# Second graph layer: the weights of two source tiles masked in one operation, scores made three steps ahead

## The chip, the core and the metric

The kernel runs on one core of a Trainium2 chip. The metric is the device time of one execution in microseconds (us). The engines are named as in the profile: PE (TensorE, matrix products), PEld (its weight loads), DVE (VectorE), ACT (ScalarE), POOL (GpSimd) and SP (the queue that issues most of the DMAs). Each engine works through its own instructions in order, and waits on semaphores for the others.

## The reference

The input has 3327 nodes with 256 features (padded in the kernel to 26 tiles of 128 rows) and a dense 0/1 adjacency matrix. Two layers follow each other; each is a graph step and a step on the rows alone (a mixture of experts in the first layer, an attention block in the second). The change touches the graph step of the second layer only:

```python
def _L1_gnn_ref(x, adj, W, a):
    Wh = x @ W
    e_src = Wh @ a[:d_out]
    e_dst = Wh @ a[d_out:]
    e = jax.nn.leaky_relu(e_src[:, None] + e_dst[None, :], 0.2)
    mask = (adj > 0) | jnp.eye(N, dtype=bool)
    e = jnp.where(mask, e, NEG_INF)
    alpha = jax.nn.softmax(e, axis=1)
    return alpha @ Wh

x = x + _L1_gnn_ref(_layernorm(x, axis=-1), adj, L1_gnn_W, L1_gnn_a)
```

For every pair of nodes there is a score, a mask from the adjacency matrix, an exponential, and the weighted sum of the rows `Wh`.

## The kernel before

**The stage.** `graph1` first makes `Wh` for all 26 tiles (`wh`, with a column of ones behind, so that the sum of the weights comes out of the same product). Then it walks over the matrix: `steps` lists the pairs (b, j), with b one of seven blocks of up to four target tiles (the last block has two) and j one of the 26 source tiles, j running fastest. That makes 182 steps. All of a step's work is in four small functions, and the loop at lines 747 to 772 calls them with leads of different length.

**A step's four parts.** `weights(k)` (line 681) makes a tile u of 128 x 512 (128 x 256 in the last block): one DVE operation adds the source's term `d8` to the block's first row, and takes the maximum with the block's second row, which is the leaky ReLU; then ACT takes the exponential in place, with `d2` as its bias. The two rows `bcast[b]` are the same on all partitions and are made once for a block. `masked(k)` (line 692) is one DVE operation that compares the adjacency panel with zero and takes the minimum with u: where there is no edge, the weight is 0. Its result is the tile p. `gather(k)` (line 703) is up to four products on PE, p of each target tile against `wh` of the source tile, summed over the 26 steps in PSUM (one accumulator for each target tile). u and p each have four buffers (`ep`, line 617).

**The leads.** Each engine's instructions are issued in the order of the program (`InOrder`). In step k the loop issues `weights(k + 2)`, then `masked(k + 1)`, then `gather(k)`. So on DVE the order is u, p, u, p, and the two scores of the next steps are under way when a step is masked.

**What else shares the engines.** For each tile of the next block `top` (a custom DVE operation over 128 x 1664, twice a tile) finds the largest source term among its neighbours; ACT makes its input with a `Sign` (`sign`, same width). `top` runs in the odd steps 1 to 15 (in block 5 only 1 to 7, as block 6 has two tiles), `sign` two or three steps earlier. `finish` closes a tile of the block before in the steps 1 to 4: a reciprocal and one DVE operation that waits for PE's last product of that tile, then a DMA issued by POOL. `shifts`, at step 16, makes the shift of the next block with small DVE operations, and POOL makes `dg` from it; at step 18 PE multiplies it (`rows`), at step 21 ACT copies it out (`spread_rows`). `panel` loads four source tiles of the adjacency matrix with up to four DMAs on SP, and POOL puts ones on the diagonal where the panel holds one. From block 3 on, POOL also prepares a table (`igw`) for the stage that follows.

## Time and profile before

| what | value |
|---|---|
| median of 6 runs | 2937.1 us (2934.43 to 2941.73) |
| the profiled execution | 2938.11 us, of which the span of the profile is 2936.4 us |
| the stage of the 182 steps | from 622.1 us (first u) to 974.5 us (last product) |
| u on DVE, 128x512 / 128x256 | 156 and 26 operations, 788 and 491 ns each on average |
| exponential of u on ACT, 128x512 / 128x256 | 156 and 26 operations, 718 and 508 ns |
| p on DVE, 128x512 / 128x256 | 156 and 26 operations, 740 and 438 ns |
| `top` on DVE in the stage | 44 operations, 1914 ns |
| `sign` on ACT in the stage | 44 operations, 1574 ns |
| products of `gather` on PE | 1352 passes (676 products of two passes), 310.0 us busy |

Times are of one execution. In the rows of the profile, `out<-in` names the tiles, `xN` counts, and the number in brackets is the idle time of the engine before the row and what ended it. All rows carry line 61, because a helper there issues every instruction; the tile names tell them apart: `u<-bc,d` is the score, `u<-u,d` its exponential, `p<-pan,u` the masking, `sg<-sg,dst` is `top`, `acc<-wh,p` the products. An instruction's duration reaches a little over the start of the next one on the same engine.

### The profile page before, as it was taken

Reading aid. Unit: us, or ns where it says so; the run is one execution under the profiler, and the core shown is the slowest. Engines: PE = TensorE matmul, PEld = TensorE weight load, DVE = VectorE, ACT = ScalarE, POOL = GpSimd, SP = SyncE. Lnnn points to the kernel's source line nnn. Section 1 sums busy time; section 2 is a strip of 40 time slices with the busy share of each in tenths; the row PEclk is TensorE's granted clock in tenths of the full one; section 3 lists DMA queues with packets and bytes.
Section 4 is the critical chain, followed back from the end, with each engine's and each line's share of the span. In section 5 each row is a group of like instructions: output and inputs, shape, how many; then the busy total and the mean of one; then the engine's idle time right before and its main releaser. Section 6 shows DMA issues by size and latency. Waiting matters only on the chain. (4 is left out here: it accounts for less than half of the span.)

```text
span 2936.4 us, 125324 instructions
## 1 busy us (share of the span) xinstructions
PE 2650.9 (90%) x53422; PEld 1961.6 (67%) x53422; DVE 2397.7 (82%) x5619; ACT 1810.7 (62%) x5128; POOL 973.4 (33%) x1448
## 2 busy tenths in 40 slices
PE   7999998879989798999999999999999999999995
PEld 5878887757767666666666666666666666666664
DVE  5102643589999587889989999999999999999997
ACT  6420135555554477777777777777667767676774
POOL 6441634522142146544334323323122222122121
PEclk9999989999999799999999999999999999999998
DMA  9994568647775232333333433333333433433332
GB/s 378 358 328 137 186 206 279 206 177 265 269 243 181 71 91 78 115 99 114 117 100 112 121 110 113 113 115 115 117 112 113 118 111 115 120 113 109 116 110 78
DMA packets 258189, 449.70 MB, mean 153 GB/s; under 512 B 58817, under 2 KB 156609, under 8 KB 257505
## 3 DMA queue, kind: packets, MB, share of 16 engines
q1 hardware_dynamic: 245536, 417.50, 45.3%
q0 software_dynamic: 6576, 18.02, 1.6%
q8 instruction: 421, 6.90, 1.0%
q10 hardware_dynamic: 5520, 6.18, 0.7%
q14 instruction: 136, 1.11, 0.1%
HBM read 393.37 MB, written 25.88 MB: 143 GB/s over the span
## 5 line engine op out<-in xcount | busy, mean ns | idle before, releaser
L61 ACT ACTIVATE sc<-sc,anmax 128x512 f32<-128x512 f32 (+3 forms) x1568 | 1039.8, 668 | 108.6 <-DVE anmax L61 108.5
L61 PEld LDWEIGHTS po<-sc,vr 32*64 32x64 f32 x43728 | 660.1, 130 | 389.2 <-DVE sc L61 233.6
L61 PE MATMUL po<-sc,vr 32*64 32x128 f32 x43728 | 761.8, 275 | 112.7 <-DVE sc L61 75.6
L61 DVE STREAM_TRANSPOSE sc<-sc 128x2048 f32<-128x2048 f32 (+3 forms) x392 | 816.4, 2083 | 27.1 <-ACT sc L61 26.2
L61 PE MATMUL pqk<-kt,qt 64*128 64x512 f32 (+1 forms) x2944 | 737.7, 582 | 21.0 <-ACT qt L61 6.8
L61 DVE TENSOR_SCALAR_CACHE_REDUCE sc<-pqk 128x512 f32<-128x512 f32 (+2 forms) x1152 | 654.9, 622 | 49.1 <-PE pqk L61 47.6
L61 PEld LDWEIGHTS pqk<-kt,qt 64*128 64x128 f32 x2944 | 298.5, 186 | 233.0 <-issue 102.5
L61 PE MATMUL acc<-wh,p 128*128 128x259 f32 x1352 | 310.0, 387 | 34.8 <-DVE p L61 34.7
L61 PEld LDWEIGHTS acc<-wh,p 128*128 128x128 f32 x1352 | 254.2, 190 | 92.9 <-DVE p L61 52.4
L61 PE MATMUL acc<-y,pan 128*128 128x256 f32 x1352 | 302.5, 384 | 11.2 <-DMA pan<-in_adjt_dram 9.4
L61 POOL TENSOR_TENSOR ot<-ot,sxd 128x512 f32<-128x512 f32 x83 | 105.7, 1274 | 584.2 <-ACT ot L61 572.2
L61 ACT ACTIVATION_READ_ACCUMULATOR sc<-sc,anmax 128x1 f32 x1568 | 298.9, 191 | 0.0
L61 PEld LDWEIGHTS acc<-y,pan 128*128 128x128 f32 x1352 | 257.4, 192 | 52.1 <-issue 16.8
L61 DVE CUSTOM_DVE_ANT_0 sc<-pqk,mask 128x512 f32<-128x512 f32 (+3 forms) x416 | 242.2, 636 | 23.5 <-PE pqk L61 23.0
L61 ACT ACTIVATE u<-u,d 128x512 f32<-128x512 f32 (+1 forms) x182 | 125.2, 688 | 159.5 <-DVE u L61 159.4
L61 DVE SCALAR_TENSOR_TENSOR u<-bc,d 128x512 f32<-128x512 f32 (+1 forms) x182 | 135.6, 746 | 0.1
L61 DVE SCALAR_TENSOR_TENSOR p<-pan,u 128x512 f32<-128x512 f32 (+1 forms) x182 | 126.9, 697 | 10.3 <-PE acc L61 6.2
L61 ACT ACTIVATE junk<-ar 128x1664 bf16<-128x1664 f32 x52 | 82.7, 1591 | 64.9 <-DMA ar<-in_adj_dram 63.7
L61 ACT COPY qkv<-ptO 128x256 f32<-128x256 f32 x104 | 38.3, 368 | 133.9 <-PE ptO L61 133.7
L61 PE MATMUL ptO<-igw,ot 128*128 128x68 f32 x832 | 116.6, 283 | 4.1 <-issue 2.4
L61 PEld LDWEIGHTS ptO<-igw,ot 128*128 128x128 f32 x832 | 101.6, 192 | 22.9 <-issue 16.9
L61 DVE CUSTOM_DVE_ANT_0 sg<-sg,dst 128x1664 bf16<-128x1664 bf16 (+2 forms) x56 | 99.7, 1788 | 1.2 <-ACT dst L61 1.0
(340 smaller groups left out, 3027.5 us busy)
## 6 DMA issues: line engine op xcount, KB each, us to landing
vr<-vs SPq DMA_DIRECT2D x976, 128.0 KB
ar<-in_adj_dram SPq DMA_DIRECT2D x104, 832.0 KB
vr<-vs SPq DMA_DIRECT2D x544, 96.0 KB
pan<-in_adjt_dram SPq DMA_DIRECT2D x156, 256.0 KB
pan<-in_adjt_dram SPq DMA_DIRECT2D x26, 1024.0 KB
pan<-in_adjt_dram SPq DMA_DIRECT2D x20, 832.0 KB
w1e<-w SPq DMA_DIRECT2D x59, 256.0 KB
took<-places SPq DMA_DIRECT2D x59, 129.0 KB
```

The costliest lines, as they stand in the source:

```text
L61: made = make(*args, **kw)
```

## The change

Two steps now share one tile of u and one of p, both of shape 128 x 4 x 2 x 128: target tile, which of the two steps, target row. `weights(k)` fills one half of the shared u, in four pieces of 128 elements (two in the last block); it is still one DVE operation and one exponential for each step. `masked` is called in odd steps only, and masks both halves in one operation of 128 x 1024 (128 x 512 in the last block): the panel already holds the two source tiles side by side. The products take their halves of p. The number of elements on every engine stays as it was.

`weights` moves from two to three steps ahead, so that both halves of u exist when they are masked; before the loop, `weights(2)` is added. u and p have three buffers of the double size (24 KB for each partition in all, 16 KB before).

On DVE the order of two steps with a `top` was u(k+1), p(k), u(k+2), p(k+1), `top`, for k odd in the step of the last three. It is now u(k+2), u(k+3), p(k+1 and k+2), `top`, where u(k+2) is issued in the even step k-1 and the rest in the odd step k. What an even step has besides (`finish` in steps 2 and 4, `shifts` in step 16) stands between the two scores.

```diff
             def weights(k):
                 b, j = steps[k]
                 n = len(blocks[b]) * P
-                u = ep.tile([P, BLK], F32, tag="u", name="u")
+                if j % 2 == 0:
+                    es_[k // 2] = ep.tile([P, 4, 2, P], F32, tag="u", name="u", bufs=3)
+                u = es_[k // 2][:, : n // P, j % 2, :]
+                ab = bcast[b].rearrange("p i (t q) -> p i t q", t=4)[:, :, : n // P, :]
                 nc.vector.scalar_tensor_tensor(
-                    u[:, :n], bcast[b][:, 0, :n], d8[:, j : j + 1], bcast[b][:, 1, :n],
-                    ALU.add, ALU.max,
-                )
-                nc.scalar.activation(u[:, :n], u[:, :n], AF.Exp, bias=d2[:, j : j + 1])
-                es_[k] = u
+                    u, ab[:, 0], d8[:, j : j + 1], ab[:, 1], ALU.add, ALU.max
+                )
+                nc.scalar.activation(u, u, AF.Exp, bias=d2[:, j : j + 1])
 
             def masked(k):
+
                 b, j = steps[k]
                 n = len(blocks[b])
-                p = ep.tile([P, 4, P], F32, tag="p", name="p")
+                p = ep.tile([P, 4, 2, P], F32, tag="p", name="p", bufs=3)
 
                 nc.vector.scalar_tensor_tensor(
-                    p[:, :n, :], pans[b, j // 4][:, :n, j % 4, :], 0.0,
-                    es_.pop(k).rearrange("p (t q) -> p t q", t=4)[:, :n, :], ALU.is_gt, ALU.min,
-                )
-                ps_[k] = p
+                    p[:, :n, :, :], pans[b, j // 4][:, :n, ds(j % 4, 2), :], 0.0,
+                    es_.pop(k // 2)[:, :n, :, :], ALU.is_gt, ALU.min,
+                )
+                ps_[k], ps_[k + 1] = p[:, :, 0, :], p[:, :, 1, :]
...
             weights(0)
             weights(1)
+            weights(2)
             masked(0)
...
-                    weights(k + 2)
+                if k + 3 < len(steps):
+                    weights(k + 3)
                 if k + 3 in when:
                     sign(*when[k + 3])
-                if k + 1 < len(steps):
+                if k + 1 < len(steps) and j % 2:
                     masked(k + 1)
                 gather(k)
```

## The prediction

> **What bounds the kernel now.** I read the page's costliest groups first, to find the stage that the change touches, then the busy time of that stage in windows, then VectorE's (DVE's), ScalarE's (ACT's) and TensorE's (PE's) instructions in order of time.

> ```profile
> span 2936.4 us, 125324 instructions
> L61 PE MATMUL acc<-wh,p 128*128 128x259 f32 x1352 | 310.0, 387 | 34.8 <-DVE p L61 34.7
> L61 DVE SCALAR_TENSOR_TENSOR u<-bc,d 128x512 f32<-128x512 f32 (+1 forms) x182 | 135.6, 746 | 0.1
> L61 DVE SCALAR_TENSOR_TENSOR p<-pan,u 128x512 f32<-128x512 f32 (+1 forms) x182 | 126.9, 697 | 10.3 <-PE acc L61 6.2
> ...
> 676.00:730.00 54.00, 48.30 (x208) 38.39 (x208) 52.93 (x84) 30.00 (x35) 11.67 (x14) 1.00 0.73 255
> 920.80:974.50 53.70, 53.63 (x244) 46.06 (x244) 46.51 (x100) 24.76 (x44) 13.06 (x18) 1.00 0.34 104
> ```

> The stage runs from 622 to 975 us: 182 steps, in seven blocks of 26 (the last half as wide). The window lines give PE, weight loads, DVE, ACT, POOL. In a middle block DVE is busy 52.9 of 54.0 us and PE 48.3: DVE sets the pace. From 920.8 us to the end PE is busy 53.6 of 53.7. So what the stage loses or gains is what DVE loses or gains up to 920.8. Inside a block (DVE, ACT, then PE in a neighbouring stretch):

> ```profile
> 692.44 0.75 DVE L61 SCALAR_TENSOR_TENSOR u<-bc,d 128x512 f32<-128x512 f32 x1
> 693.11 0.68 DVE L61 SCALAR_TENSOR_TENSOR p<-pan,u 128x512 f32<-128x512 f32 x1
> 693.71 0.74 DVE L61 SCALAR_TENSOR_TENSOR u<-bc,d 128x512 f32<-128x512 f32 x1
> 694.37 0.68 DVE L61 SCALAR_TENSOR_TENSOR p<-pan,u 128x512 f32<-128x512 f32 x1
> 694.98 1.88 DVE L61 CUSTOM_DVE_ANT_0 sg<-sg,dst 128x1664 bf16<-128x1664 bf16 x1
> ...
> 693.28 0.72 ACT L61 ACTIVATE u<-u,d 128x512 f32<-128x512 f32 x1 [2.12 <-DVE u L61]
> ...
> 706.87 3.77 PE L61 MATMUL acc<-wh,p 128*128 128x259 f32 x16 [0.58 <-DVE p L61]
> 711.21 3.76 PE L61 MATMUL acc<-wh,p 128*128 128x259 f32 x16 [0.57 <-DVE p L61]
> ```

> One instruction of DVE starts before the last has quite ended, so I price by start to start: 0.66 us for a score (u), 0.60 for a masking (p), 1.81 for a `top` (694.98 to 696.79). Two steps with a `top` cost DVE 2×(0.66+0.60)+1.81 = 4.34, and PE, with 3.76 of work, waits 0.58 in each such pair. Without a `top` DVE needs 2.53 for two steps, and runs ahead until the four p buffers are full:

> ```profile
> 729.65 0.69 DVE L61 SCALAR_TENSOR_TENSOR p<-pan,u 128x512 f32<-128x512 f32 x1 [0.38 <-issue]
> 730.26 0.75 DVE L61 SCALAR_TENSOR_TENSOR u<-bc,d 128x512 f32<-128x512 f32 x1
> 731.42 0.69 DVE L61 SCALAR_TENSOR_TENSOR p<-pan,u 128x512 f32<-128x512 f32 x1 [0.41 <-PE acc L61]
> 733.16 0.69 DVE L61 SCALAR_TENSOR_TENSOR p<-pan,u 128x512 f32<-128x512 f32 x1 [0.39 <-PE acc L61]
> ```

> Here p comes every 1.75 us, the rate of PE. These gaps add up to 5.3 us in the first five blocks (14 of them), DVE's only slack.

> **The change, part by part.**

> *One masking for two steps.* 91 masked operations replace 182, with the same elements. The narrow block has the size that gives the fixed part:

> ```profile
> 957.25 0.41 DVE L61 SCALAR_TENSOR_TENSOR p<-pan,u 128x256 f32<-128x256 f32 x1
> 957.58 0.47 DVE L61 SCALAR_TENSOR_TENSOR u<-bc,d 128x256 f32<-128x256 f32 x1
> ```

> 256 elements take 0.335 us start to start, 512 take 0.602: 0.267 per 256, so 1024 should take 1.136, and a pair saves 1.204-1.136 = 0.07. By the durations (0.41, 0.68) it would be 0.14; at the other end nothing, if the wide form ran no better. I take 0.07. Up to 920.8 some 70 pairs count: -4.9 us (0 to -9.8). [...]

> *The new wait.* This is the price that the diff doesn't show. Before, a masking takes the score whose exponential was issued a whole step earlier: p and the next u lie between, 1.26 us. After, the order on DVE in an odd step is u, masking of two, `top`; the masking needs the exponential of the score just one DVE operation earlier. How long that takes is seen at the stage's first step:

> ```profile
> 622.09 1.42 DVE L61 SCALAR_TENSOR_TENSOR u<-bc,d 128x512 f32<-128x512 f32 x2
> 622.88 1.38 ACT L61 ACTIVATE u<-u,d 128x512 f32<-128x512 f32 x2 [1.22 <-DVE u L61]
> 623.69 0.69 DVE L61 SCALAR_TENSOR_TENSOR p<-pan,u 128x512 f32<-128x512 f32 x1 [0.19 <-issue]
> ```

> u ends 0.74 after its start, ACT starts 0.09 later (693.19 to 693.28 above), runs 0.72 and ends at 623.60 here, p starts 0.09 later: 0.74+0.09+0.72+0.09 = 1.64 after u's start. Two scores keep DVE for 2×0.66 = 1.325. So DVE stands 0.315 us in a pair. Bounds: with no hand-off at all 1.46-1.325 = 0.135; with forms in four pieces a little slower, 0.36. I take 0.315, since each of its parts is a row of this trace. Behind the waiting masking stand `top`, the next score and so ACT's next exponential; PE waits for all of them.

> Where it is filled: in blocks 1 to 5 the `finish` of steps 2 and 4 (0.60) comes between the two scores, and at step 16 `shifts` (1.17) does. Of the 70 pairs 55 keep the wait. Where POOL works on `pan`, `dg` or `igw`, DVE's operations are stretched (0.94 for 0.74 at 676 to 684 us), so a score behind covers more: 0.12 of wait is left. POOL is busy with these some 55 of 300 us, so 10 of the 55: 45×0.315+10×0.12 = +15.4 us.

> ACT itself isn't late: in a pair it has two exponentials and a sign, 0.63+1.49+0.63 = 2.75 of 4.6 us. In the form 128x4x128 u and its exponential write pieces of 128; the nearest row, p itself, reads `pan` in such pieces and is no slower than the flat u (0.60, 0.66). I take nothing; the bound is in a rival.

> *Three pairs of buffers.* DVE may be six steps ahead of PE where it was four. That takes the 5.3 us of gaps away if DVE can use it: after step 17 it gains 3.46-(1.325+0.315+1.136) = 0.68 in a pair, 3.4 over five pairs, which never fills three pairs; so no gaps: -5.3. Being further ahead, `finish` at step 1 comes before PE has closed the old block; following PE's steps of 1.73 from step 18 gives 0.3 us in each of four blocks: +1.2 (0 to +4).

> *Coarser hand-over.* PE gets two steps at once. At the last place where it waits (920.8, step 9 of block 5) it used to have one step ready 0.66+0.60 us ahead of the next. Now it gets both 2.53 later and does them back to back, where it would have been 1.73 on: +0.8, once.

> *Start, loads, rest.* The third score ahead puts 0.66 before the first masking, but the work is needed anyway, and DVE reaches its third u at the same time as before: nothing. The panels, rows and copies are issued at the same steps, so SP's and POOL's queues keep their order, and a panel is released a step earlier; its DMA isn't waited for by DVE now (no such releaser among its waits). Were that cover gone, POOL's diagonal fixes, 1.7 us ahead of their reader at 682.8, would be late first. Nothing of the later stage changes: 0.

> **Sum.** +15.4-4.9-5.3+1.2+0.8 = +7.2 us. The profiled execution took 2938.1 (span 2936.4 and 1.7 around it), so 2945.3; it lies 1.0 above the median of six runs, so against that median 2944.3.

> **The rivals.**

> *The wait is covered, and the kernel is faster.* Place: the masking of two behind the second score. Without it remain -4.9-5.3+0.8+1.2 = -8.2: 2928.9. It decides below about 0.15 us in a pair (55×0.15 = 8.2). For it: the bound without hand-offs is 0.135. Against: 0.09 was seen at both hand-overs. Chance 0.11.

> *The deeper buffers pay: no change.* If DVE got one more step ahead at each of five block ends, PE would begin the stretch with `top` 1.73 richer: -8.6. The waits in that stretch alone (30 pairs, some 8.5), its savings (35×0.07 = 2.5) and +0.8 give +6.8; together -1.8, with 1.2 of `finish` -0.6: 2936.5. For it: the gaps show that DVE is stopped by buffers. Against: 3.4 us of gain isn't enough to fill them. Chance 0.22.

> *Slower still.* Pieces of 128 cost: the 256-element operation on y, written in two pieces, takes 0.484 at least, the flat one 0.471; that is 0.026 per 512, 150 scores 3.9 and longer exponentials 1.4: 2949.6. In the last block a pair costs DVE 0.79+0.37+0.60 = 1.76 against PE's 1.73, so that PE, covered now, might wait up to 1.8: 2951.4. The masking that doesn't save at all (the change then not doing what it says) gives 2949.2. Chance 0.17.

> **How the numbers follow.** The forecast has 0.50. A difference of 0.2%, 5.9 us, is about what a measurement of this kernel can tell. Of the forecast 0.39 lies beyond that and 0.11 below; of the second rival 0.17 is within, 0.04 slower and 0.01 faster; the first is faster; the third slower. Slower 0.60, same 0.28, faster 0.12. Range 2935 to 2953: it takes in the second and third rivals and leaves out the first and a little above. The forecast alone has 2941 to 2949.

> **What would show it.** Between two scores in a row and the wide p an idle of about 0.3 us with ACT's u as releaser, in 50 or more pairs, absent where `finish` or `shifts` lies between the scores; p of 1024 elements near 1.2 us; no p waiting for PE in blocks 0 to 4; PE waiting over 0.8 us in each pair with a `top`; the stage ending some 7 us later, and the later stage as long as before. I am wrong if the idle is under 0.15 us, if PE's waits vanish, or if u's or the exponential's duration moves.

## The result, and the profile after

The changed kernel takes 2946.55 us (median of 38 runs, 2934.47 to 2952.95), the kernel before 2940.95 us in the runs beside them (77 runs): a ratio of 1.0017, 95% interval 1.0011 to 1.0023. That is 5 us slower (3.2 to 6.8). The profiled execution took 2949.97 us.

The costliest groups on the page of the changed kernel (busy us, mean ns of one, then idle time before and its releaser):

```profile
span 2948.3 us, 125048 instructions
L61 PE MATMUL acc<-wh,p 128*128 128x259 f32 x1352 | 313.9, 391 | 37.5 <-DVE p L61 37.4
L61 DVE SCALAR_TENSOR_TENSOR u<-bc,d 128x512 f32<-128x512 f32 (+1 forms) x182 | 131.2, 753 | 0.1
L61 DVE SCALAR_TENSOR_TENSOR p<-pan,u 128x1024 f32<-128x1024 f32 (+1 forms) x91 | 111.8, 1228 | 15.8 <-PE acc L61 4.9
```

91 maskings take 111.8 us where 182 took 126.9, but DVE now stands 15.8 us before them (10.3 before). How much the stage loses, and on which engine, a window shows from the first score to the last place where PE waits for weights (stretch, then busy time of PE, weight loads, DVE, ACT, POOL, then PE's granted clock). The kernel before:

```profile
622.00:920.80 298.80, 264.80 (x1132) 212.62 (x1132) 291.35 (x455) 164.99 (x194) 65.40 (x72) 0.99 0.73 252
```

and the changed kernel:

```profile
623.50:931.50 308.00, 271.36 (x1140) 219.39 (x1140) 291.37 (x388) 166.49 (x196) 71.63 (x72) 0.97 0.71 244
```

The two stretches end 1.73 us apart in PE's work (the changed kernel hands over two steps there, the kernel before one). DVE is busy for the same 291 us, and idle for 16.6 us in place of 7.4. By this count all that was lost is DVE standing still. From the first u to the last reciprocal the stage takes 360.1 us, against 352.6 before: 7.5 more.

Where DVE stands: two steps with a `top`, on DVE of the changed kernel (start, duration):

```profile
696.35 1.41 DVE L61 SCALAR_TENSOR_TENSOR u<-bc,d 128x512 f32<-128x512 f32 x2
697.88 1.22 DVE L61 SCALAR_TENSOR_TENSOR p<-pan,u 128x1024 f32<-128x1024 f32 x1
699.02 1.88 DVE L61 CUSTOM_DVE_ANT_0 sg<-sg,dst 128x1664 bf16<-128x1664 bf16 x1
...
700.83 1.41 DVE L61 SCALAR_TENSOR_TENSOR u<-bc,d 128x512 f32<-128x512 f32 x2
```

with ACT between them:

```profile
697.13 0.72 ACT L61 ACTIVATE u<-u,d 128x512 f32<-128x512 f32 x1 [2.05 <-DVE u L61]
```

The exponential starts 0.78 us after its score and ends at 697.85; the wide masking starts at 697.88, 1.53 after that score, where two scores alone would need 1.325. So it waits 0.21 us, and the pair takes 4.48 us (4.34 before). The same kernel's DVE at the end of a block:

```profile
848.16 1.23 DVE L61 SCALAR_TENSOR_TENSOR p<-pan,u 128x1024 f32<-128x1024 f32 x1 [0.52 <-ACT u L61]
...
851.68 1.22 DVE L61 SCALAR_TENSOR_TENSOR p<-pan,u 128x1024 f32<-128x1024 f32 x1 [0.96 <-PE acc L61]
853.79 0.17 DVE L61 RECIPROCAL rd<-acc 128x1 f32<-128x1 f32 x1 [0.89 <-PE acc L61]
```

The gaps for PE, which I had forecast to vanish, are larger than before: over the first five blocks 3.2 us in front of p, 4.1 in front of the reciprocal of `finish`, and 1.8 in rows like the first one beyond their usual 0.13; together 9.1 against 5.3. PE says why. First the kernel before at step 18 of block 1, then the changed kernel at steps 16 to 18 of block 1 and at step 18 of block 3:

```profile
718.83 2.02 PE L61 MATMUL acc<-wh,p 128*128 128x259 f32 x8 [1.26 <-DVE p L61]
...
717.12 3.76 PE L61 MATMUL acc<-wh,p 128*128 128x259 f32 x16 [0.72 <-DVE p L61]
723.41 2.01 PE L61 MATMUL acc<-wh,p 128*128 128x259 f32 x8 [2.53 <-DVE p L61]
...
837.40 3.57 PE L61 MATMUL acc<-wh,p 128*128 128x259 f32 x8 [2.52 <-DVE p L61]
840.77 2.05 PE L61 MATMUL pb<-dg,ones 128*128 128x512 f32 x4
```

Before step 18 PE stands 2.5 us (1.26 before). DVE hands over the steps 16 and 17 together, and until it hands over 18 and 19 it has a `top`, two scores, `shifts` and a wide masking to do: 6.3 us, for which PE has 3.76 of work. The masking itself is slow here, 1.99 us from start to start (721.29 to 723.28) in place of 1.14, while POOL makes `dg`:

```profile
721.29 2.06 DVE L61 SCALAR_TENSOR_TENSOR p<-pan,u 128x1024 f32<-128x1024 f32 x1
...
720.79 3.46 POOL L61 TENSOR_TENSOR dg<-ident,ab 128x512 f32<-128x512 f32 x2 [27.06 <-DVE ab L61]
```

To the usual 0.72 this adds 0.85, and `shifts` adds its 1.17 less the wait of 0.21 that it covers: 2.53 in all. The start of PE's long uninterrupted stretch is late by this. In blocks 0, 2, 3 and 4, not in block 1, PE also runs at half its clock for a while after the stop (3.57 for 2.01 in the row of block 3; the last section has the clock). In exactly these four blocks p later waits for PE (0.30, then 0.96 three times), and the waits for PE at the end of a block are 1.5 to 2.4 us in sum; in block 1 they are 0.59.

### The profile page after: what moved, and what is told of

Read it like the earlier page. It is cut to its first block, busy times and chain, and to the rows that moved or that the text cites. A ratio compares the mean times of both kernels' runs of the same rounds, so it can differ in the third digit from the quotient of the medians.

```text
span 2948.3 us, 125048 instructions
## 1 busy us (share of the span) xinstructions
PE 2655.1 (90%) x53422; PEld 1967.2 (67%) x53422; DVE 2395.0 (81%) x5528; ACT 1810.6 (61%) x5128; POOL 983.0 (33%) x1448
## 5 line engine op out<-in xcount | busy, mean ns | idle before, releaser
L61 ACT ACTIVATE sc<-sc,anmax 128x512 f32<-128x512 f32 (+3 forms) x1568 | 1039.8, 668 | 108.5 <-DVE anmax L61 108.4
L61 PEld LDWEIGHTS po<-sc,vr 32*64 32x64 f32 x43728 | 660.3, 131 | 394.4 <-DVE sc L61 233.6
L61 PE MATMUL po<-sc,vr 32*64 32x128 f32 x43728 | 763.1, 275 | 118.3 <-DVE sc L61 73.9
L61 DVE STREAM_TRANSPOSE sc<-sc 128x2048 f32<-128x2048 f32 (+3 forms) x392 | 816.5, 2083 | 28.2 <-ACT sc L61 27.4
L61 PE MATMUL pqk<-kt,qt 64*128 64x512 f32 (+1 forms) x2944 | 735.6, 581 | 18.2 <-DVE fgs L61 4.6
L61 DVE TENSOR_SCALAR_CACHE_REDUCE sc<-pqk 128x512 f32<-128x512 f32 (+2 forms) x1152 | 654.9, 623 | 48.4 <-PE pqk L61 46.8
L61 PEld LDWEIGHTS pqk<-kt,qt 64*128 64x128 f32 x2944 | 298.7, 185 | 228.4 <-issue 100.9
L61 PE MATMUL acc<-wh,p 128*128 128x259 f32 x1352 | 313.9, 391 | 37.5 <-DVE p L61 37.4
L61 PEld LDWEIGHTS acc<-wh,p 128*128 128x128 f32 x1352 | 258.4, 193 | 94.3 <-DVE p L61 52.1
L61 PE MATMUL acc<-y,pan 128*128 128x256 f32 x1352 | 303.6, 385 | 11.8 <-DMA pan<-in_adjt_dram 10.1
L61 POOL TENSOR_TENSOR ot<-ot,sxd 128x512 f32<-128x512 f32 x83 | 105.9, 1275 | 585.9 <-ACT ot L61 574.2
L61 ACT ACTIVATION_READ_ACCUMULATOR sc<-sc,anmax 128x1 f32 x1568 | 298.7, 190 | 0.0
L61 PEld LDWEIGHTS acc<-y,pan 128*128 128x128 f32 x1352 | 257.9, 192 | 53.3 <-issue 17.8
L61 DVE CUSTOM_DVE_ANT_0 sc<-pqk,mask 128x512 f32<-128x512 f32 (+3 forms) x416 | 242.2, 637 | 24.6 <-PE pqk L61 24.3
L61 ACT ACTIVATE u<-u,d 128x512 f32<-128x512 f32 (+1 forms) x182 | 124.1, 688 | 167.2 <-DVE u L61 166.6
L61 DVE SCALAR_TENSOR_TENSOR u<-bc,d 128x512 f32<-128x512 f32 (+1 forms) x182 | 131.2, 753 | 0.1
L61 DVE SCALAR_TENSOR_TENSOR p<-pan,u 128x1024 f32<-128x1024 f32 (+1 forms) x91 | 111.8, 1228 | 15.8 <-PE acc L61 4.9
L61 ACT ACTIVATE junk<-ar 128x1664 bf16<-128x1664 f32 x52 | 82.7, 1591 | 65.0 <-DMA ar<-in_adj_dram 63.9
L61 PE MATMUL ptO<-igw,ot 128*128 128x68 f32 x832 | 117.4, 284 | 3.2 <-issue 1.5
L61 ACT COPY qkv<-ptO 128x256 f32<-128x256 f32 x104 | 38.3, 369 | 132.9 <-PE ptO L61 132.7
L61 PEld LDWEIGHTS ptO<-igw,ot 128*128 128x128 f32 x832 | 102.4, 193 | 21.9 <-issue 15.0
L61 DVE CUSTOM_DVE_ANT_0 sg<-sg,dst 128x1664 bf16<-128x1664 bf16 (+2 forms) x56 | 99.7, 1789 | 1.2 <-ACT dst L61 1.0
```

The lines of the kernel that those rows point to most:

```text
L61: made = make(*args, **kw)
```

## The experiments

All runs were compared with the kernel before on the same chip. The whole time moves by more than the effect (the median of the kernel before lay between 2940 and 2951 us from one group of runs to the next), so I read the stage too, from the first u to the last reciprocal of each profile, and profiled the kernel before again to see how far that repeats.

| run | stage, us | pair with `top`, us | PE's stop at `shifts`, us | ratio to before, 95% interval |
|---|---|---|---|---|
| before, twice | 352.6, 352.4 | 4.34 | 1.26 | |
| changed | 360.1 | 4.48 | 2.53 | 1.0017 (1.0011 to 1.0023) |
| e1_four_ahead | 351.8 | 4.27 | 2.52 | 1.0000 (0.9988 to 1.0013) |
| e2_two_masks | 355.3 | 4.34 | 2.60 | 1.0002 (0.9989 to 1.0015) |
| e3_mask_before_score | 398.6 | 5.15 | not read | 1.0156 (1.0135 to 1.0176) |
| e4_shifts_later | 353.1 | 4.49 | 0.72 | 0.9993 (0.9981 to 1.0006) |
| e5_top_between | 351.8 | 4.27 | 2.53 | 0.9998 (0.9986 to 1.0009) |
| e6_top_between_shifts_later | 345.2 | 4.27 | 0.51 | 0.9975 (0.9965 to 0.9986) |
| e7_and_finish_later | 345.5 | 4.27 | 0.50 | 0.9982 (0.9967 to 0.9997) |
| e8_before_shifts_later | 350.4 | 4.34 | 0.78 | 0.9985 (0.9975 to 0.9995) |
| e9_best_with_two_masks | 345.9 | 4.34 | 0.57 | 0.9975 (0.9964 to 0.9986) |
| e10_best_with_two_pairs | 352.5 | 4.27 | 0.51 | 0.9992 (0.9982 to 1.0002) |
| e11_before_six_buffers | 351.4 | 4.34 | 1.27 | 0.9994 (0.9984 to 1.0004) |

**The repeat.**

> The kernel before, profiled once more, on the chip of these runs: how far the stage's length repeats. If it lies within 1 us of 352.6, differences of 2 us between single profiles of the stage mean something, though the whole time moves by several us from run to run.

It took 352.4 us. So I read differences of 2 us between stages. That is shown for the kernel before only, whose PE clock is full (1.00) from 630 us to the end of the stage. Where the clock falls in between (in the changed kernel eight products then take 3.25 to 3.57 us in place of 2.01), the number of falls moves the stage too, and those kernels were profiled once.

**Scores four ahead.** One line of the changed kernel, and `weights(3)` before the loop:

```diff
-                if k + 3 < len(steps):
-                    weights(k + 3)
+                if k + 4 < len(steps):
+                    weights(k + 4)
```

> Scores made four steps ahead instead of three, everything else as in the changed kernel: the score whose exponential the wide masking needs is then two scores old. Theory A (the loss is the wait of the masking for the exponential of the score just before it, 0.21 us in a pair by the changed kernel's trace): the idle before the wide masking goes to 0, a pair with a top falls from 4.49 to 4.28 us (4.34 before), and the kernel is 0.2 to 0.4% faster than before, ratio 0.996 to 0.998. Theory B (the loss is the coarse hand-over: PE gets two steps at once and stands longer): nothing of that changes, ratio stays at 1.001 to 1.002.

The wide masking follows its scores without a wait; DVE in this run:

```profile
702.10 1.42 DVE L61 SCALAR_TENSOR_TENSOR u<-bc,d 128x512 f32<-128x512 f32 x2
703.43 1.22 DVE L61 SCALAR_TENSOR_TENSOR p<-pan,u 128x1024 f32<-128x1024 f32 x1
...
730.09 1.42 DVE L61 SCALAR_TENSOR_TENSOR u<-bc,d 128x512 f32<-128x512 f32 x2 [0.62 <-ACT bc L61]
```

The pair takes 4.27 us and the stage is 8.3 us shorter than the changed kernel's, so the wait is real, as theory A says. But the ratio missed its range: PE's stop is still there, and the next block's first score now waits 0.62 us for its rows (last line), in each of five blocks. Nor is all of the 8.3 the wait. In the changed kernel PE releases the first accumulator of a block 16.20 to 16.44 us after the end of the masking behind `shifts` where its clock fell after the stop (blocks 0, 2, 3 and 4), and 14.76 where it didn't (block 1). In this run it is 16.30 in block 0, 16.45 in block 3 and 14.75 or 14.76 in the other three. From that I take it, as an estimate, that the clock fell after two stops in this profile, against four.

**Two maskings.** The same order, each pair masked in two operations:

```diff
-                nc.vector.scalar_tensor_tensor(
-                    p[:, :n, :, :], pans[b, j // 4][:, :n, ds(j % 4, 2), :], 0.0,
-                    es_.pop(k // 2)[:, :n, :, :], ALU.is_gt, ALU.min,
-                )
+                u = es_.pop(k // 2)
+                for i in range(2):
+                    nc.vector.scalar_tensor_tensor(
+                        p[:, :n, i, :], pans[b, j // 4][:, :n, j % 4 + i, :], 0.0,
+                        u[:, :n, i, :], ALU.is_gt, ALU.min,
+                    )
```

> Order and buffers of the changed kernel, but each pair is masked by two operations of 512 elements, one after the other. Theory A: the first needs an exponential that is long done and takes 0.60 us, so the second doesn't wait: the wait (0.21) goes and the saving (0.07) too, a pair with a top takes 4.34 us again; ratio 0.999 to 1.000. Theory B: PE can begin with the first half 0.6 us sooner, so its stops shrink too, but the wait stays where it was; ratio between 1.000 and 1.0015. A third theory, that the pieces of 128 in score and exponential cost: nothing changes, 1.0015.

The pair is back at 4.34 and the stage 4.8 us shorter. The pieces of 128, the third theory, are thereby cleared of all but little; the ratio decides nothing between A and B.

**The wait made larger.** `masked(k + 1)` is issued ahead of `weights(k + 3)`.

> The suspected wait made larger: in the odd step the wide masking is issued before the newer score, so that no score lies behind the one that it waits for. Theory A: 1.53 us from the score's start to the masking's, of which only 0.7 is work: an idle of 0.8 us in place of 0.13 to 0.2, a pair with a top 4.49+0.66 = 5.15 us; 45 to 55 pairs give +25 to +36 us on the changed kernel, ratio 1.010 to 1.014. Theory B: PE's hand-over is even a little earlier, ratio 1.002 or less.

DVE in this run:

```profile
709.48 1.23 DVE L61 SCALAR_TENSOR_TENSOR p<-pan,u 128x1024 f32<-128x1024 f32 x1 [0.79 <-ACT u L61]
...
714.63 1.23 DVE L61 SCALAR_TENSOR_TENSOR p<-pan,u 128x1024 f32<-128x1024 f32 x1 [0.79 <-ACT u L61]
```

Idle 0.79 us and a pair of 5.15, both as forecast by A; the stage grows by 38.5 us, a little above its range. B falls as the only cause.

**Shifts later.** In the changed kernel, `if j == 16` becomes `if j == 17`, so that `shifts` comes behind the wide masking of that step.

> The small operations that make the next block's shifts go from step 16 (between the two scores) to step 17, behind the wide masking. In the changed kernel PE stands 2.5 us at this place in each of five blocks, and its next products then run at half speed for a time in two of them. Theory A: DVE's work is the same and this pair's wait is no longer covered (+0.2 each, 1 us in all), so nothing or slightly slower: ratio 1.001 to 1.003. Theory B: PE's stop falls from 2.5 to about 1.3 us and the slow products go; 5 x 1.2 us gained, ratio 0.999 to 1.000.

Here A falls as the only cause. PE in this run:

```profile
720.75 3.76 PE L61 MATMUL acc<-wh,p 128*128 128x259 f32 x16 [0.72 <-DVE p L61]
725.24 2.01 PE L61 MATMUL acc<-wh,p 128*128 128x259 f32 x8 [0.72 <-DVE p L61]
727.97 1.13 PE L61 MATMUL pb<-dg,ones 128*128 128x512 f32 x2 [0.72 <-POOL dg L61]
729.42 1.12 PE L61 MATMUL pb<-dg,ones 128*128 128x512 f32 x2 [0.32 <-POOL dg L61]
```

The stop falls by 1.8 us in each of five blocks, 8.9 in all. The half clock doesn't occur behind the stop of block 1 (eight products take 2.01 us), and I take it for gone in the others: the mean clock of PE over 279.6 us from the first score is 0.99, against 0.96 in the changed kernel. From the first product of step 18 to that of step 19 PE took 5.0 to 5.3 us in four blocks of the changed kernel and 3.57 in block 1, so 6.5 go (the expectation had seen two of the four). But PE now waits for POOL's `dg`, and the same stretch takes 5.14 in each block, 7.8 back. That gives 7.6, and the stage is 7.0 us shorter, though DVE's pair is as long as before the move. On DVE no p waits for PE any more in the first five blocks, and `finish` waits 1.2 us in place of 4.1.

**Top between the scores, then both, then finish.** The wait is covered by work that is there anyway: `top` goes from the end of the odd step to the next even step.

```diff
+                if k - 1 in when:
+                    top(*when[k - 1], PARTS[1])
...
-                if k in when:
-                    top(*when[k], PARTS[1])
...
-                    if j == 16:
+                    if j == 17:
                         dg = shifts(b + 1)
-                    if j == 18:
+                    if j == 19:
                         pb = rows(b + 1, dg)
```

The first two parts are the first run, all of it the second; the third moves `finish` two steps on as well.

> The changed kernel with each top moved from the end of its odd step to the next even step, where it lies between the two scores and covers the exponential (1.81 us). From the first score to the last reciprocal the stage took 352.6 us before, 360.1 in the changed kernel, 351.9 with scores four ahead, 353.1 with the shifts later. Theory A (the wait behind the second score): no idle before the wide masking in pairs with a top, 4.28 us for such a pair, and the stage is 6 to 9 us shorter than the changed kernel's, 351 to 354 us. Theory B (coarse hand-over at step 17): PE still stands 2.5 us there, and the stage stays near 360. If both cost, as the runs so far suggest, A's number holds and B's 2.5 us remain visible.

> As the run with top between the scores, and the shifts behind the wide masking of step 17, with PE's product for the rows one step later (step 19) so that it doesn't wait for POOL. If the two costs are separate, their gains add up: 360.1-7-7 = 346 us for the stage, ratio 0.997 to 0.998. If both act through one limit (DVE's sum of work, with gaps where PE stops it), the second brings less than 3 us: 349 to 352.

> As the run before it, and finish moved from steps 1 to 4 to steps 3 to 6, since its reciprocal waits 0.3 to 0.9 us for PE's last products in each block when DVE is further ahead. If these waits are slack that DVE has anyway, nothing changes; if they are lost, 5 x 0.5 to 0.9 = 2.5 to 4.5 us are gained: a stage of 342 to 345 us if the run before it takes 346.

The first shortens the stage by 8.3 us and leaves PE's 2.5, as A said; the second takes another 6.6 off. So the two moves add up. The 8.3 again holds more than the wait: the mean clock over 279.6 us from the first score is 0.97 in place of 0.96, and up to step 9 of block 5 DVE waits 4.9 us for PE in place of 7.3. DVE in the second:

```profile
699.20 0.75 DVE L61 SCALAR_TENSOR_TENSOR u<-bc,d 128x512 f32<-128x512 f32 x1
699.87 1.22 DVE L61 SCALAR_TENSOR_TENSOR p<-pan,u 128x1024 f32<-128x1024 f32 x1
701.00 0.75 DVE L61 SCALAR_TENSOR_TENSOR u<-bc,d 128x512 f32<-128x512 f32 x1
701.66 1.89 DVE L61 CUSTOM_DVE_ANT_0 sg<-sg,dst 128x1664 bf16<-128x1664 bf16 x1
```

In a pair with a `top` no idle is left. This version is faster than the kernel before, 2933.5 us against 2940.25, and with that than the changed one. Moving `finish` brought nothing: in the second run its reciprocal doesn't wait in blocks 1 to 5, so there was nothing to gain, and the run doesn't show whether such waits are slack.

**What the gain consists of.** Four controls: the shifts later in the kernel before; the best version with two maskings; the best version with `bufs=2` for p; and the kernel before with `bufs=6` for p.

> A control on the kernel before: single maskings, scores two ahead, but shifts at step 17 behind the masking and the rows' product at step 19, as in the best version so far (stage 345.2 us, against 352.6 and 352.4 in two profiles of the kernel before). If the place of the shifts is a gain of its own, without the merged masking, the stage falls to 348 or less. If it only repairs what the pairs broke, the stage stays at 352 to 354: PE gets one step there as it did, and DVE's work is the same.

> The best version so far (top between the scores, shifts at step 17, three pairs of buffers) with each pair masked by two operations of 512 elements: what the merge alone is worth once neither wait nor hand-over costs. By the rows of 0.60 and 1.14 us, 0.07 us in some 70 pairs: a stage 4 to 5 us longer, 349 to 350.5. If the merge is worth nothing, 345 to 346.

> The best version so far with two pairs of buffers for the masked weights instead of three, so that DVE may be four steps ahead of PE as in the kernel before. My prediction gave the third pair 5.3 us (the gaps in which DVE waited for PE to release a buffer). If that holds, p waits for PE at the end of each block again, 1 us or more in each, and the stage is 350 to 352. If the depth is worth little, below 347.

> The kernel before with six buffers for p instead of four, and nothing else: single maskings, scores two ahead, shifts at step 16. In the best version so far the third pair of buffers was worth 7.3 us of the stage (352.5 to 345.2) and the merged masking 0.7 (345.9 to 345.2). If the gain is the depth's alone, the gaps of 0.4 us in which p waits for PE go, and the stage falls from 352.5 to 346 to 348 us, ratio 0.997 to 0.9985. If the depth only pays with pairs or with the moved shifts, the stage stays above 350.

The place of the shifts alone gives 2.1 us, between the two expectations. The merge is worth only 0.7, against 4 to 5 expected. Its steps without a `top` show the reason. The best version's DVE:

```profile
720.62 1.22 DVE L61 SCALAR_TENSOR_TENSOR p<-pan,u 128x1024 f32<-128x1024 f32 x1
721.77 1.41 DVE L61 SCALAR_TENSOR_TENSOR u<-bc,d 128x512 f32<-128x512 f32 x2
723.30 1.23 DVE L61 SCALAR_TENSOR_TENSOR p<-pan,u 128x1024 f32<-128x1024 f32 x1
```

and the same place with two maskings:

```profile
722.26 1.28 DVE L61 SCALAR_TENSOR_TENSOR p<-pan,u 128x512 f32<-128x512 f32 x2
723.47 1.44 DVE L61 SCALAR_TENSOR_TENSOR u<-bc,d 128x512 f32<-128x512 f32 x2
724.82 1.29 DVE L61 SCALAR_TENSOR_TENSOR p<-pan,u 128x512 f32<-128x512 f32 x2
```

2.68 us for a wide pair, 2.56 for two single ones: here nothing covers the exponential. Eight pairs in a block save 0.07 each and five lose 0.12, which leaves nothing.

The third pair of buffers is worth 7.3 us in the best version. With two, DVE stops for PE at the end of each block:

```profile
726.73 1.23 DVE L61 SCALAR_TENSOR_TENSOR p<-pan,u 128x1024 f32<-128x1024 f32 x1 [0.74 <-ACT u L61]
730.24 1.23 DVE L61 SCALAR_TENSOR_TENSOR p<-pan,u 128x1024 f32<-128x1024 f32 x1 [0.96 <-PE acc L61]
```

But in the kernel before, six buffers alone gave only 1.1 us, not the 4 to 6 that I expected. Its DVE:

```profile
730.87 0.69 DVE L61 SCALAR_TENSOR_TENSOR p<-pan,u 128x512 f32<-128x512 f32 x1 [0.41 <-ACT u L61]
733.65 0.17 DVE L61 RECIPROCAL rd<-acc 128x1 f32<-128x1 f32 x1 [0.82 <-PE acc L61]
```

p waits for PE no more, but 0.41 us for an exponential and then 0.82 in `finish`: the gap has moved. In these runs depth pays only where nothing else stops DVE a little later. Not run: six buffers and the moved `shifts` together in the kernel before, without pairs.

## Why the prediction was right, and where it was not

The sign was right, and so was the wait as a cause; that the size came so near was partly luck: +7.2 us forecast, 5.0 (3.2 to 6.8) measured, 7.5 in the profiled stage, and the time lies in the range. It ended within the 0.2% that I had given 0.28. Single steps fared worse than the sum, and so did my signs. The wide p takes 1.23 us and its releaser is ACT's u, as I said, and the median score and exponential are as long as before (0.74 and 0.72). But the idle stands in the rows as 0.13, under the 0.15 at which I had called myself wrong (from start to start it is 0.21, and my 0.315 was counted so); p does wait for PE, in four blocks; and PE waits 0.72 in the usual pair, not over 0.8.

*The merged masking, -4.9.* 1.14 us from start to start was right (697.88 to 699.02), and a pair without a wait took 4.27, 0.07 below 4.34. So the larger saving by durations, 0.14, was rightly not taken: the wide masking lasts 1.22 us, and the next row starts 1.14 after it. Two maskings made the stage 4.8 us shorter in the changed order, and 0.7 longer in the best version.

*The new wait, +15.4.* Right in place and releaser, mis-sized: 0.21 us and not 0.315, because the exponential started 0.78 us after its score (0.83 with another operation behind it, the row I took) and the masking 0.03 after the exponential (0.09). The first number stood in a row that I showed: 622.09 to 622.88. And it stands in some 40 pairs up to step 9 of block 5, not in 55: 8.4 us, an estimate. Covering it in the pairs with a `top` gave 8.3 us of stage, of which 2.4 are shorter waits for PE.

*Three pairs of buffers, -5.3 and +1.2.* This step failed: "which never fills three pairs; so no gaps". DVE stood for 9.1 us in place of 5.3, 4.1 of them in `finish`, where I had 1.2. With a smaller wait DVE gained 3.46-2.68 = 0.78 in a pair instead of 0.68, and PE began its stretch later; but block 1 has both and filled no buffer. What it lacks is the fall of PE's clock (1.00 from 723.4 to 725.3 us, where block 3 has 0.54 from 837.4 to 840.9). Three more runs bear this out: in e1_four_ahead p waits for PE in blocks 0 and 3 (0.56 and 0.96 us), just the two with the later release, and in e4_shifts_later and e6_top_between_shifts_later, whose mean clock over 279.6 us from the first score is 0.99, nowhere in the first five blocks.

*Coarser hand-over, "+0.8, once".* This step failed too, and it is the larger miss: it holds at every place where PE waits (0.72 us in the usual pair in place of 0.58, 2.53 at `shifts` in place of 1.26), and between the hand-over of steps 16 and 17 and the next DVE has `top`, `shifts` and, beside POOL's `dg`, a masking of 1.99 us in place of 1.14. I had counted `shifts` there as cover for a wait of 0.3 us; PE stood 1.27 us longer in each block, and in four blocks ran slow behind it (eight products in 3.25 to 3.57 us), which is what filled the buffers. Moving `shifts` gave 7.0 us. In the kernel before, moving `shifts` (and the rows' product) one step on gives 2.1, so some 5 of the 7.0 belong to the pairs, an estimate.

So the forecast was close because a wait priced nearly twice too high and a hand-over priced nearly at nothing balanced: that is luck. Counted on DVE, as an estimate: 8.4 for the wait, -4.9 for the merging (70 pairs at the 0.07 measured), and 9.1-5.3 = +3.8 for its stops at PE, where the forecast had 15.4, -4.9 and -5.3+1.2+0.8 = -3.3. The sum is +7.3, and the stage shows 7.5; the two errors are -7.0 and +7.1.

The rivals: the faster case isn't met in its condition, and its price of -8.2 without the wait didn't hold either: with the wait covered in the pairs with a `top` and nothing else changed, the stage is 0.7 us shorter than before (e1, e5), and -7.3 came only when PE's stop went too (e6). The deeper buffers do pay 7 us, once DVE can use them.

What stays open: whether the stage's 7.5 us of one profile and the 5.0 of the timed runs differ by chance, as the rest of the kernel moves by several us from profile to profile (2583.8 and 2587.7 in the two of the kernel before), and how many falls of PE's clock the changed kernel has in other executions.

## What to carry to other kernels

When two operations are merged on an engine, look at what each half waited for: the merged one waited for the later input here (0.21 us in a pair) and handed over the earlier half late where its reader had caught up (PE stood 2.53 us in place of 1.26). Give the input one more operation of distance, or put unrelated work between; here moving `top` and `shifts` by one step turned 5 us lost into 7 gained, and most of that is the deeper buffers, not the merge.

## What the hardware showed that I had not expected

After a stop of 2.52 us PE ran at half its clock. Windows of the changed kernel (the column after POOL's count is the granted clock):

```profile
836.00:837.00 1.00, 0.00 (x0) 0.00 (x0) 1.00 (x1) 0.19 (x1) 1.00 (x2) 1.00 0.00 0
...
838.00:839.00 1.00, 1.00 (x3) 0.76 (x3) 1.00 (x2) 0.17 (x1) 0.94 (x3) 0.50 0.49 109
839.00:840.00 1.00, 1.00 (x4) 0.76 (x3) 1.00 (x2) 0.86 (x2) 0.94 (x3) 0.50 0.98 352
840.00:841.00 1.00, 1.00 (x4) 0.81 (x3) 1.00 (x2) 0.41 (x1) 0.93 (x2) 0.50 0.94 297
```

The clock is 0.50 for 3.4 us, from 837.7 to 841.1, and eight products take 3.57 us that take 2.01 elsewhere. It followed the stop in four of the five blocks (eight products in 3.46, 3.45, 3.57 and 3.25 us), and not in block 1, at 723.4 us, with a stop as long.

```profile
721.61:725.03 3.42, 1.62 (x7) 1.43 (x8) 3.42 (x3) 0.78 (x2) 2.64 (x2) 1.00 0.17 37
725.03:728.44 3.41, 3.41 (x13) 2.23 (x12) 3.15 (x5) 2.18 (x4) 0.00 (x0) 1.00 0.98 310
...
776.29:779.70 3.41, 0.89 (x4) 0.45 (x4) 3.39 (x5) 0.72 (x1) 3.07 (x2) 0.99 0.35 144
779.70:783.12 3.42, 3.42 (x9) 2.46 (x8) 3.29 (x4) 1.44 (x2) 0.39 (x1) 0.51 0.85 268
```

In block 2 the stop lies in one stretch, PE is busy 0.89 us of it, and the next stretch has half the clock; blocks 3 and 4 have 0.89 too, block 0 has 1.34. In block 1 the grid cuts the stop in two, PE is busy 1.62 us of the emptier stretch, and the clock stays. So the stretch ahead of a fall wasn't idle here: 1.34 us of work stood in one. A border between 1.34 and 1.62 isn't shown. Outside the stage the changed kernel's clock fell at 609.0 us after a stretch with 1.61, and that of the kernel before fell at 995.1 after one with 1.92 and stayed full at 612.8 after one with 1.43. As the ends of products are modelled, these sums are estimates. The first step of the grid behind the first u comes 0.98 us after it in the kernel before and 2.59 in the changed one. Whether a stop of 2.5 us costs these us more looks like chance, which is my estimate: it did in four of five blocks here, and by PE's release in two of five in e1_four_ahead.
